# Two-layer transformer on one core: half of the second sequence's rows turned by VectorE and moved by DMA, and the last weights loaded later from another queue

## The chip, the core and the metric

The kernel runs on one core of a Trainium2 chip. The metric is the time of one execution on the device in microseconds (us); lower is better. The engines of the core run side by side and meet through semaphores: TensorE (PE in the profile; PEld is its load of stationary operands), VectorE (DVE), ScalarE (ACT), GpSimd (POOL) and SyncE (SP). SP and POOL each have a queue from which they issue DMA transfers in order; an instruction that waits holds up everything behind it on its own engine.

## What is computed

The input x is 2 sequences of 512 rows by 512 columns, in float32. Two layers follow, each an attention and a feed-forward, each with a residual and a layer norm behind it:

```
x = layernorm(x + L0_attn(x))     # linear attention, 8 key heads
x = layernorm(x + L0_ffn(x))      # ternary weights, 512 -> 1376 -> 512, int8 rounding
x = layernorm(x + L1_attn(x))     # this section is touched
x = layernorm(x + L1_ffn(x))      # down(silu(x gate) * (x up)), 512 -> 1376 -> 512

def L1_attn(x):                   # one head of width 128
    q, k, v = split(x @ Wqkv + bqkv)            # Wqkv is 512 x 384
    p = softmax(q @ k.T / sqrt(128))            # 512 x 512 for each sequence
    return (p @ v) @ Wo + bo
```

## The kernel before, in words

Every sequence is four tiles of 128 rows, `xs[b][t]` (b = 0, 1; t = 0 to 3), with the 512 columns along the free dimension. A product contracts over the partitions, so before every projection the rows have to be turned: x^T is held as four blocks k of 128 columns by 512 rows. The kernel turns rows in two ways.

- **On TensorE**: a 128x128 transpose against the identity, four to a PSUM bank, and then a copy of the bank to SBUF by ScalarE or VectorE (`transposed`, L128 to L130; L981 and L983).
- **In squares**: VectorE's transpose instruction turns each 32x32 square of a tile in place (`squares`), and `move_squares` (L305 to L322) then carries the squares to their places: for 16 pairs of 32-partition groups, 8 DMAs from SP (L316), 4 from POOL (L316), and the 4 on the diagonal, which stay in their partitions, as copies on VectorE (L320).

The stage of this study is where the second layer's attention begins, with the end of the first feed-forward ahead of it:

1. The first feed-forward's down products (L848) are finished row tile by row tile: ScalarE scales and truncates (L865, L170, L171), VectorE adds the residual (L881, L885) and takes the statistics (L138, L140), POOL makes the reciprocal root (`rstd`, L146 and L147), and VectorE applies the norm (L152, `normed`). Sequence 1's tiles come last, tile 3 at the very end.
2. Second attention, sequence 0: tiles 0 and 1 were turned in squares (L963 and L316), tiles 2 and 3 on TensorE (L981). `pqk` (L1148) makes q and k in two halves of 256 rows; `pv` (L1166) makes v, and VectorE adds its bias (L1172); `psc` (L1099) makes four tiles of scores; VectorE takes the maxima (L1105, L1106), ScalarE the exponentials `prob` (L1121), and VectorE turns those in squares (L1180), which are then moved (`pt_p`, L316).
3. Second attention, sequence 1: all four tiles are turned on TensorE (`pt_a`, L128, 16 transposes of 128x128) and copied by ScalarE and VectorE (L130); `pqk` runs over 512 rows at a time; then v, the scores and the exponentials.
4. `pot` (L1213, values times probabilities of sequence 0), `pt_p` (L128, the turning of sequence 1's probabilities on TensorE), `po` (L1230, the output projection of sequence 0), and so on into the last feed-forward (L1383, L1338).

The output projection bias `bo` is added to the rows ahead of the attention's result: for sequence 0 by POOL (L1181), for sequence 1 by accumulating DMAs from POOL's queue (L1196), which wait until `pt_p` has landed (L1194).

The last feed-forward's weights are `gu` (gate and up, chunks 0 to 10, 512 KB each, the last 384 KB) and `wd` (down, 11 chunks of 256 KB, the last 192 KB). All are loaded from SP's queue: `gu` 6 to 10 first, then, behind the moves of sequence 0's squares (`moves_a`), `wd` 0 to 10 (L256) and `gu` 0 to 5 (L245). The feed-forward uses them in the order 6, 7, 8, 9, 10, 0, 1, ... 5: ScalarE and VectorE split each chunk in parts (L1026, L1036, L1037) ahead of its products.

What sets the order: on ScalarE, VectorE, TensorE and SP a scheduler orders instructions by the program and by the ties written into it (`tc.issue_after(a)` holds the instructions under it behind `a`); POOL keeps the program's order. PSUM has eight banks, taken in turn (`psum(name)`, `bufs=8`): the ninth tile waits until the first has been read. The pool `xtp` has two slots of 128 x 2048 float32, tag `xt`, which sequence 1's turned rows, the turned probabilities (`xt_p1`) and the squares of the last feed-forward's rows (`squares_r1`) take in turn.

```
for half in range(2 - b):                 # L1140: q and k
    for j in range(2):
        for k in range(NK):
            if b: p, rows = pqk[j], xt[:, k, :]                       # 512 rows
            else: p = pqk[j].rearrange(...)[:, half]; rows = xt_a10[half][:, :, k, :]
            nc.tensor.matmul(p, wqkv[:, k, ts(j, D)], rows, ...)      # L1148
```

Of the kernel before, what the change touches and what calls it, by code (L numbers as in the profile page):

```python
# [10 lines left out]
F32 = mybir.dt.float32  # L11
# [8 lines left out]
P = 128  # L20
B, S, HID = 2, 512, 512
NT = S // P
# [17 lines left out]
def kernel(  # L40
# [195 lines left out]
    def branch(flag):  # L236
        return nc.values_load(flag[0:1, 0:1], engines=[PE], min_val=0, max_val=1)

    def up_weights(gu_in, name, chunks=range(len(CHUNKS))):
        gus = []  # L240
        for c in chunks:
            i, n = CHUNKS[c]
            gu = wffn.tile([P, 2, NK, n], F32, tag=f"gu{c}", name=f"gu{name}_{c}")
            at = 2 * HID * i
            nc.sync.dma_start(  # L245
                gu.rearrange("p a k i -> p (a k i)"),
                gu_in[at : at + 2 * HID * n].rearrange("(p f) -> p f", p=P),
            )
            gus.append(gu)
        return gus  # L250

    def down_weights(wd_in, name):
        wds = []
        for c, (i, n) in enumerate(CHUNKS):
            wd = wdp.tile([P, HID], F32, tag=f"wd{c}", name=f"wd{name}_{c}")
            nc.sync.dma_start(wd[:n], wd_in[i : i + n, :])  # L256
            if n < P:
                nc.gpsimd.memset(wd[n:], 0.0)
            wds.append(wd)
        return wds  # L260
# [497 lines left out]
    moved = move_squares(squares, xt1)  # L758
    wdp = ctx.enter_context(tc.tile_pool(name="wdp", bufs=1))
    with tc.issue_after(moved.ins):  # L760
        wds = down_weights(wd0_in, "0")
    with tc.tile_pool(name="f0", bufs=2) as f0:
        factors = {}

# [105 lines left out]
        def added(i, behind=(), late=(), first=()):  # L870
            b, t = order[i]
            with ExitStack() as tied:
                for step in behind:
                    tied.enter_context(tc.issue_after(step.ins))
                ta, tb = truncated_parts(f0, ys[i], P, f"d{i}")

            x = xs[b][t]
            with ExitStack() as tied:
                for step in first:
                    tied.enter_context(tc.issue_after(step.ins))  # L880
                nc.vector.scalar_tensor_tensor(x, tb, 128.0, x, ALU.min, ALU.subtract)  # L881
            with ExitStack() as tied:
                for step in late:
                    tied.enter_context(tc.issue_after(step.ins))
                taken[i] = nc.vector.scalar_tensor_tensor(x, x, -1.0, ta, ALU.mult, ALU.add)  # L885
            stats[i] = layernorm_stats(x, f"f0_{i}")
# [16 lines left out]
        def normed(i, behind=None):  # L903

            b, t = order[i]
            n = min(i + 1, len(order) - 1)
            if behind is None:
                behind = taken[n if t == NT - 1 else f"f0_{n}"]

            with tc.issue_after(behind.ins):  # L910
                norms.append(layernorm_apply(xs[b][t], xs[b][t], stats[i]))
            return norms[-1]
# [65 lines left out]
        for t in range(TURNED, NT):  # L978
            pt = psum(f"pt_a10_{t}")
            for k in range(NK):  # L980
                nc.tensor.transpose(pt[:, ts(k, P)], xs[0][t][:, ts(k, P)], ident)  # L981
            copies.append(
                nc.scalar.copy(xt_a10[1][:, t - TURNED], pt.rearrange("p (k i) -> p k i", k=NK))  # L983
            )
        added(i - 2)
        normed(i - 3)
        added(i - 1, behind=copies[-2:])
        normed(i - 2)
        for i in range(len(order), len(order) + 2):
            f0_down(i)  # L990

    def joined_weights(gu_in, c):

# [12 lines left out]
        nc.sync.dma_start(half.rearrange("p (k i) -> p k i", k=NK), up[:, :, : P // 2])  # L1006
        return full, half

    gus = up_weights(gu1_in, "1", range(6, len(CHUNKS) - 1))
    gus.append(joined_weights(gu1_in, len(CHUNKS) - 1))  # L1010
    with tc.issue_after(moves_a.ins):
        wds = down_weights(wd1_in, "1")
    gus = up_weights(gu1_in, "1", range(6)) + gus

# [73 lines left out]

    probs = []

    def scores(b):

        qt, kt, _ = qkv[b]
        got = []
        for t in range(NT):
            p = psum(f"psc_{b}_{t}")
            nc.tensor.matmul(p, qt[:, ts(t, P)], kt, start=True, stop=True)  # L1099
            got.append((p, small.tile([P, 1], F32, tag="mx", name=f"mx_{b}_{t}", bufs=8)))  # L1100

        def maxima(tiles):
            for t in tiles:
                p, mx = got[t]
                nc.vector.reduce_max(mx, p, AX.X)  # L1105
                done = nc.vector.tensor_scalar_mul(mx, mx, -scale)  # L1106
            return done

        return got, maxima
# [18 lines left out]
    qkv = []  # L1128
    for b in range(B):
        if b:  # L1130
            xt = transposed(xs[b], f"a1{b}")
            with tc.issue_after(copies[-2].ins), tc.issue_after(copies[-1].ins):
                split_up(0, room0)
                split_up(1, room1[:6])
        qk = []
        qk2 = query_tile(f"qk_{b}")
        if b == 0:
            v2 = query_tile("v")
        pqk = [psum(f"pqk_{b}_{j}") for j in range(2)]
        for half in range(2 - b):  # L1140
            for j in range(2):
                for k in range(NK):
                    if b:
                        p, rows = pqk[j], xt[:, k, :]
                    else:
                        p = pqk[j].rearrange("p (h t i) -> p h t i", h=2, i=P)[:, half]
                        rows = xt_a10[half][:, :, k, :]
                    nc.tensor.matmul(  # L1148
                        p, wqkv[:, k, ts(j, D)], rows,
                        start=(k == 0), stop=(k == NK - 1),  # L1150
                    )
        for j, p in enumerate(pqk):
            s = qk2[:, j, :]
            moved = nc.scalar.activation(s, p, AF.Identity, bias=bqk[:, j : j + 1])
            qk.append(s)
        if b:
            pt0 = fp.tile([P, NT, NK, P], F32, tag="it10", name="pt_p0", bufs=1)
            move_squares(squares, pt0)
            pt0 = pt0.rearrange("p t k i -> p k t i")
        else:  # L1160
            table(AF.Exp, moved)
        v = v2[:, b, :].rearrange("p (t d) -> p t d", t=NT)
        for t in range(NT):
            p = psum(f"pv_{b}_{t}")
            for k in range(NK):
                nc.tensor.matmul(  # L1166
                    p[:, :D],
                    xt[:, k, ts(t, P)] if b else xt_a10[t // 2][:, t % 2, k, :],
                    wqkv[:, k, ts(2, D)],
                    start=(k == 0), stop=(k == NK - 1),  # L1170
                )
            nc.vector.tensor_add(v[:, t, :], bv, p[:, :D])  # L1172
        qkv.append((qk[0], qk[1], v))
        if b == 0:
            got, maxima = scores(0)
            maxima(range(NT))
            exponentials(0, got)
            squares = fp.tile([P, NT, HID], F32, tag="it00", name="squares_p0", bufs=1)
            for t in range(NT):
                nc.vector.transpose(squares[:, t, :], probs[0][0][t])  # L1180
                nc.gpsimd.tensor_add(xs[0][t], xs[0][t], bo)  # L1181
# [364 lines left out]
    for i, (b, j) in enumerate(steps):  # L1546
        held.append(up1(b, j, held))
        finished = held[0][0]
        if i == AHEAD:
            with tc.issue_after(in_turn.last.ins), tc.issue_after(uppers.ins):  # L1550
                moved = finish_up()
        elif i > 1:
            while len(held) > 1:
                moved = finish_up()
        if i == 1:
            in_turn(lambda: split_up(AHEAD - 1, take(6)))
        elif i == 2:
            rooms[1] = rows_room(1, "r1")
            x3[1] = row_blocks(rooms[1])
            for k in range(NK):  # L1560
                with tc.issue_after(in_turn.last.ins):
                    uppers, in_turn.last = rows_from_squares(k)
        elif i == AHEAD:
            for h, m, d in x3[1]:
                in_turn(lambda: crossed(d, h, m))
        with tc.issue_after(moved.ins):
            if ahead <= last and finished == 1:
                split_up(
                    ahead, room0 if ahead == AHEAD else take(6 if turn[ahead] < last else 4)
                )  # L1570
                ahead += 1
            for _ in range(2):
                if len(down_parts) <= last and len(free) >= (15 if ahead <= AHEAD + 3 else 9 if ahead <= last else 3):
                    split_down()
        if (b, j) == (1, last - 1):
            quarters = [split_tile(0, 0)]
# [69 lines left out]
```

## Time and profile before

| | us |
|---|---|
| median of 4 runs | 454.68 |
| lowest and highest of them | 454.58, 455.06 |
| the profiled execution | 454.54 |
| its span, first to last instruction | 452.8 |
| TensorE busy in it | 445.8 (98%) |
| VectorE, ScalarE, POOL busy | 318.0 (70%), 259.5 (57%), 118.1 (26%) |
| TensorE's share of the chain that ended last | 97% |

Times in the profile are counted from the start of the span. A line of the timeline gives the start, the length, the engine, the line of code, the operation and what it writes and reads, the count where several are merged, and in square brackets the idle time before it and what ended that. Float32 products appear as two TensorE instructions each, so a product of 128x512 counts twice ("x8" for four of them). The ends of TensorE's instructions are modelled, so one starts before the one ahead of it has drained; the chain of work gives net times.

### The profile page before, as it was taken

How to read it: one execution, taken by the hardware profiler on the slowest of the kernel's cores; microseconds unless marked ns; L12 is line 12 of the kernel's file. 1: busy time of each engine (PE TensorE's matmuls, PEld its weight loads, DVE VectorE, ACT ScalarE, POOL GpSimd, SP SyncE). 2: the span in 40 equal slices, each digit the busy share in tenths (PEclk: the TensorE clock that was granted, in tenths of full speed). 3: DMA queues.
4: the chain of work that ended last, by engine and by line, in shares of the span. 5: the costliest groups of instructions: out<-in, count | busy, mean ns of one | idle time of the engine just before them, and what ended most of it. 6: DMA issues, size and time to landing. Idle time of an engine off the chain costs nothing.

```text
span 452.8 us, 5850 instructions
## 1 busy us (share of the span) xinstructions
PE 445.8 (98%) x1913; PEld 337.1 (74%) x1913; DVE 318.0 (70%) x634; ACT 259.5 (57%) x493; POOL 118.1 (26%) x164
## 2 busy tenths in 40 slices
PE   8999999999999999999999999999999999999995
PEld 8887753444587888888885578888888888888884
DVE  3976757877886898859898889545535447777524
ACT  5788995567467975567755645454645456442311
POOL 0400206565640059203384137000000000012111
PEclk9999999999999999999999999999999999999999
DMA  8999980020038001132693503200000000000101
GB/s 305 396 265 314 190 306 7 0 46 4 1 58 262 5 2 48 48 94 46 185 371 73 90 1 51 43 0 1 0 1 0 0 3 0 0 25 23 48 25 68
DMA packets 35604, 38.57 MB, mean 85 GB/s; under 512 B 23024, under 2 KB 23920, under 8 KB 35568
## 3 DMA queue, kind: packets, MB, share of 16 engines
q1 hardware_dynamic: 32912, 31.31, 21.2%
q0 software_dynamic: 2368, 6.42, 7.7%
q8 instruction: 22, 0.36, 0.3%
q10 hardware_dynamic: 288, 0.36, 0.2%
q14 instruction: 14, 0.11, 0.1%
HBM read 32.45 MB, written 2.10 MB: 76 GB/s over the span
## 4 chain that ended last, share of the span: by engine, by line
PE 97%; issue 1%; DVE 0%; ACT 0%; POOL 0%; POOLq 0%
PE pu L1338 24%; PE po L593 12%; PE pd L1338 12%; PE pq L538 9%; PE pg_f L789 9%; PE pu_f L789 9%; PE pd_f L848 4%; PE pqk L1148 3%; PE pu L1383 2%; PE pv L1166 2%; PE pot L1213 2%; PE po L1230 2%; PE psc L1099 2%; PE pmw L579 2%; PE pq L509 1%
## 5 line engine op out<-in xcount | busy, mean ns | idle before, releaser
L593 PE MATMUL po<-mw,q 128*128 128x512 f32 x128 | 56.9, 598 | 0.0
L1338 PE MATMUL pu<-r,ugu 128*128 128x512 f32 x200 | 48.6, 389 | 0.0
L146 POOL TENSOR_TENSOR rstd_f<-mv_f,ln_eps 128x1 f32<-128x1 f32 x15 | 6.0, 397 | 161.8 <-DVE mv_f L1506 128.8
L364 ACT ACTIVATE pu<-pu 128x512 f32<-128x512 f32 x42 | 24.2, 580 | 41.4 <-PE pu L1338 37.6
L593 PEld LDWEIGHTS po<-mw,q 128*128 128x128 f32 x128 | 22.8, 189 | 32.5 <-issue 15.9
L1338 PEld LDWEIGHTS pu<-r,ugu 128*128 128x128 f32 x200 | 37.5, 188 | 7.8
L615 DVE SCALAR_TENSOR_TENSOR x<-po,den,x 128x511 f32<-128x511 f32 x40 | 29.8, 746 | 1.9
L170 ACT ACTIVATE ta_f<-y_f,below_half 128x512 int8<-128x512 f32 (+1 forms) x22 | 15.9, 722 | 24.6 <-DVE y_f L158 21.8
L610 POOL TENSOR_TENSOR y<-y,y 128x511 f32<-128x511 f32 x16 | 21.3, 1332 | 24.6 <-ACT y L606 23.9
L1338 PE MATMUL pu<-r,it_early 128*128 128x512 f32 x104 | 24.9, 389 | 0.0
L1397 DVE TENSOR_TENSOR it_f<-ev,pu 128x512 f32<-128x512 f32 x20 | 13.7, 684 | 15.7 <-PE pu L1338 15.4
L1226 ACT ACTIVATE x<-x,off_f,rstd_f 128x512 f32<-128x512 f32 x7 | 5.7, 816 | 31.6 <-POOL off_f L1225 31.6
L815 DVE SCALAR_TENSOR_TENSOR it_f<-tb_f,ta_f 128x512 fp32r<-128x512 int16 (+1 forms) x22 | 15.6, 707 | 11.1 <-ACT tb_f L171 11.1
L1338 PEld LDWEIGHTS pu<-r,it_early 128*128 128x128 f32 x104 | 19.5, 188 | 4.1
L1338 PE MATMUL pd<-ugu,r 128*128 128x512 f32 (+1 forms) x79 | 22.5, 362 | 0.0
L789 PE MATMUL pg_f<-x,tu 128*128 128x512 f32 x88 | 22.1, 393 | 0.0
L789 PE MATMUL pu_f<-x,tu 128*128 128x512 f32 x88 | 21.7, 389 | 0.0
L376 POOL TENSOR_SCALAR td<-wd,inv_down 128x512 fp32r<-128x512 f32 x11 | 20.4, 1872 | 3.2 <-DVE inv_down L206 3.2
L848 PE MATMUL pd_f<-td,it_f 128*128 128x512 f32 x88 | 20.3, 389 | 0.0
L597 ACT ACTIVATE den<-po,den_eps 128x1 f32<-128x1 f32 x64 | 14.1, 272 | 10.6 <-PE po L593 10.5
L789 PEld LDWEIGHTS pg_f<-x,tu 128*128 128x128 f32 x88 | 16.4, 188 | 4.0 <-DVE x L615 0.4
L789 PEld LDWEIGHTS pu_f<-x,tu 128*128 128x128 f32 x88 | 16.5, 188 | 3.5
(396 smaller groups left out, 1118.5 us busy)
## 6 DMA issues: line engine op xcount, KB each, us to landing
gu<-in_gu SPq DMA_DIRECT2D x20, 512.0 KB, 6.7
wd<-in_wd SPq DMA_DIRECT2D x20, 256.0 KB, 5.4
wo<-in_wo SPq DMA_DIRECT2D x8, 512.0 KB, 8.6
wo<-in_wo POOLq DMA_DIRECT2D x8, 512.0 KB, 9.4
wq<-in_wq SPq DMA_DIRECT2D x8, 256.0 KB, 4.5
x<-in_x SPq DMA_DIRECT2D x7, 256.0 KB, 4.4
out<-x SPq DMA_DIRECT2D x7, 256.0 KB, 2.0
x<-in_bo POOLq DMA_DIRECT2D x4, 256.0 KB, 6.1
```

What stands on the lines that cost most here:

```text
L170: nc.scalar.activation(a[:n], y, AF.Relu, bias=below_half[:n])
L364: return nc.scalar.activation(p, p, AF.Copy, scale=BIG + 1.0)
L376: eng.tensor_scalar(out, w, factor, None, ALU.mult)
L538: done = nc.tensor.matmul(p, w, x, start=(start and i == 0), stop=(i == len(todo) - 1), skip_group_check=not start,)
L593: nc.tensor.matmul(po, qs[b][h0 + j][:, ts(t, P)], mw[:, h0 + j, :], start=True, stop=True,)
L597: nc.scalar.activation(den[:, j : j + 1], po[:, LAST:], AF.Identity, bias=den_eps)
L610: nc.gpsimd.tensor_add(ys[0][:, :LAST], ys[0][:, :LAST], y[:, :LAST])
L615: steps.append(nc.vector.scalar_tensor_tensor(x[:, :LAST], four[j][:, :LAST], d, x[:, :LAST], ALU.mult, ALU.add))
L789: nc.tensor.matmul(pp[a], t[:, a, i % NK, :], x2[b][i], start=(i == 0), stop=(i == 2 * NK - 1),)
L815: nc.vector.scalar_tensor_tensor(it[:n], tb[:n], 128.0, ta[:n], ALU.min, ALU.subtract)
L848: nc.tensor.matmul(pd, inter[b][c][:, ts(t, P)], td[c].bitcast(F32R), start=(c == 0), stop=(c == last),)
L1338: done = nc.tensor.matmul(p, w, x, start=(start and i == 0), stop=(i == n - 1), skip_group_check=not start,)
```

## The change

It does two things.

First, sequence 1's tiles 0 and 1 are turned in squares by VectorE inside the end of the first feed-forward, each behind the norm of its tile, and `move_squares` carries them to `xt_a11` (8 DMAs from SP, 4 from POOL, 4 copies on VectorE). Tiles 2 and 3 are still turned on TensorE, 8 transposes instead of 16, but earlier: between the first and the second score tile of sequence 0 (`turn_others`), with both copies on ScalarE. The q and k products of sequence 1 then run in two halves of 256 rows, tiles 2 and 3 first.

Second, of the last feed-forward's weights only `gu` 0 and 1 stay on SP behind the moves (now the moves of sequence 1's squares); `gu` 2 to 5 and all of `wd` are issued from POOL's queue, inside the last feed-forward, behind a small POOL copy `landed_r1` that waits for the last block of sequence 1's turned rows.

```diff
@@ end of the first feed-forward
+        squares_a = xtp.tile([P, NT, HID], F32, tag="xt", name="squares_a11")
+        xt_a11 = xtp.tile([P, NT, NK, P], F32, tag="xt", name="xt_a11")
         added(i - 2)
-        normed(i - 3)
+        last_norm = normed(i - 3)
+        with tc.issue_after(last_norm.ins):
+            done = nc.vector.transpose(squares_a[:, 0, :], xs[1][0])
         added(i - 1, behind=copies[-2:])
-        normed(i - 2)
+        with tc.issue_after(done.ins):
+            last_norm = normed(i - 2)
+        with tc.issue_after(last_norm.ins):
+            nc.vector.transpose(squares_a[:, 1, :], xs[1][1])
         for i in range(len(order), len(order) + 2):
             f0_down(i)
+        moves_a = move_squares(squares_a[:, :TURNED], xt_a11[:, :TURNED])
@@ the last feed-forward's weights
-    gus = up_weights(gu1_in, "1", range(6, len(CHUNKS) - 1))
+    gus = [None] * 6 + up_weights(gu1_in, "1", range(6, len(CHUNKS) - 1))
     gus.append(joined_weights(gu1_in, len(CHUNKS) - 1))
     with tc.issue_after(moves_a.ins):
-        wds = down_weights(wd1_in, "1")
-    gus = up_weights(gu1_in, "1", range(6)) + gus
+        gus[:2] = up_weights(gu1_in, "1", range(2))
@@ second attention
+    def turn_others(t):
+        if t != 1:
+            return
+        for t in range(TURNED, NT):
+            pt = psum(f"pt_a11_{t}")
+            for k in range(NK):
+                nc.tensor.transpose(pt[:, ts(k, P)], xs[1][t][:, ts(k, P)], ident)
+            copies.append(nc.scalar.copy(xt_a11[:, t], pt.rearrange("p (k i) -> p k i", k=NK)))
...
         if b:
-            xt = transposed(xs[b], f"a1{b}")
...
-        for half in range(2 - b):
+        xt = [xt_a11[:, :TURNED], xt_a11[:, TURNED:]] if b else xt_a10
+        for half in (1, 0) if b else (0, 1):
...
-            got, maxima = scores(0)
+            got, maxima = scores(0, turn_others)
@@ last feed-forward, behind the split of sequence 1's rows
+            landed = small.tile([P, 1], F32, tag="off", name="landed_r1")
+            nc.gpsimd.tensor_copy(landed[:SQ], x3[1][NK - 1][0][:SQ, S - 1 :].bitcast(F32))
+            gus[2:6] = up_weights(gu1_in, "1", range(2, 6), nc.gpsimd)
+            wds = down_weights(wd1_in, "1", nc.gpsimd)
```

The order of the changed kernel's instructions, which the scheduler fixes when the kernel is built, is this. VectorE: the transpose of tile 0 stands right behind the residual of tile 2 (L885), the transpose of tile 1 right behind that of tile 3, and one of the four diagonal copies ahead of tile 3's last statistics, three behind its norm, all ahead of the v additions of sequence 0. ScalarE: the two new copies stand ahead of the first exponential; three of the splits of the first weights stand between the first and the second exponential, where they stood behind the fourth. POOL: the four moves stand behind the last reciprocal root and ahead of the `bo` additions. TensorE: as told above, with no other move. From the output projection on, all engines but POOL and SP have the order that they had.

More of the change, by code (lines that the diff above doesn't have):

```diff
@@ L237, in branch, with up_weights @@
         return nc.values_load(flag[0:1, 0:1], engines=[PE], min_val=0, max_val=1)
-    def up_weights(gu_in, name, chunks=range(len(CHUNKS))):
+    def up_weights(gu_in, name, chunks, eng=nc.sync):
         gus = []
@@ L244, in up_weights @@
             at = 2 * HID * i
-            nc.sync.dma_start(
+            eng.dma_start(
                 gu.rearrange("p a k i -> p (a k i)"),
@@ L250, in up_weights, with down_weights @@
         return gus
-    def down_weights(wd_in, name):
+    def down_weights(wd_in, name, eng):
         wds = []
@@ L255, in down_weights @@
             wd = wdp.tile([P, HID], F32, tag=f"wd{c}", name=f"wd{name}_{c}")
-            nc.sync.dma_start(wd[:n], wd_in[i : i + n, :])
+            eng.dma_start(wd[:n], wd_in[i : i + n, :])
             if n < P:
@@ L760 @@
     with tc.issue_after(moved.ins):
-        wds = down_weights(wd0_in, "0")
+        wds = down_weights(wd0_in, "0", nc.sync)
     with tc.tile_pool(name="f0", bufs=2) as f0:
@@ L1091, with scores @@
     probs = []
-    def scores(b):
+    def turn_others(t):
[6 more added lines that the diff above has]
+            copies.append(nc.scalar.copy(xt_a11[:, t], pt.rearrange("p (k i) -> p k i", k=NK)))
+    def scores(b, between=lambda t: None):
         qt, kt, _ = qkv[b]
@@ L1097, in scores @@
         for t in range(NT):
+            between(t)
             p = psum(f"psc_{b}_{t}")
@@ L1139 @@
         pqk = [psum(f"pqk_{b}_{j}") for j in range(2)]
-        for half in range(2 - b):
+        xt = [xt_a11[:, :TURNED], xt_a11[:, TURNED:]] if b else xt_a10
+        for half in (1, 0) if b else (0, 1):
             for j in range(2):
                 for k in range(NK):
[L1143 to L1147, printed above, removed]
+                    p = pqk[j].rearrange("p (h t i) -> p h t i", h=2, i=P)[:, half]
+                    rows = xt[half][:, :, k, :]
                     nc.tensor.matmul(
@@ L1167 @@
                     p[:, :D],
-                    xt[:, k, ts(t, P)] if b else xt_a10[t // 2][:, t % 2, k, :],
+                    xt[t // TURNED][:, t % TURNED, k, :],
                     wqkv[:, k, ts(2, D)],
```

## The prediction

> **What bounds the kernel.** I read the page's busy shares first (TensorE 98%), then TensorE's waits over the whole span:
>
> ```profile
> engine line waited for: us in total, times, longest us
> PE rise L113 <- DVE below_half L108: 1.1, 1, 1.1
> PE pq L509 <- ACT xt_raw L484: 0.2, 1, 0.2
> ```
>
> TensorE waits 1.3 us in all, at the very start. From then until 441.9 us it never stops, so the time falls only by TensorE work that is taken away, and rises by any wait that is put in. Next, the chain of work from 215 to 275 us, which gives net times:
>
> ```profile
> 221.13 0.87 PE pt_a L981 x8
> 222.01 6.91 PE pqk L1148 x32
> 228.92 3.57 PE pv L1166 x32
> 232.49 3.44 PE psc L1099 x8
> 235.92 1.75 PE pt_a L128 x16
> 237.67 7.03 PE pqk L1148 x16
> 244.70 3.57 PE pv L1166 x32
> 248.27 3.44 PE psc L1099 x8
> 251.71 3.43 PE pot L1213 x8
> 255.14 1.75 PE pt_p L128 x16
> 256.88 3.44 PE po L1230 x8
> ```
>
> The lines at 235.92 and 237.67, sequence 1's transposes and its q and k, are what the change touches; sequence 0 has the same work in the new form at 221.13 and 222.01.
>
> **What is taken away.** Sixteen transposes cost 1.75 us (235.92). Eight stay, and eight cost 0.87 us (221.13): **-0.88 us**. The q and k products over 512 rows took 7.03 us, in halves of 256 rows they took 6.91 us for sequence 0: **-0.12 us**. Together -1.00 us, and nothing else is removed from TensorE, so this is the most that the change can bring. All the rest is whether TensorE comes to wait. I walk the changed order through the old durations; times without a row are estimates made in this way.
>
> **VectorE up to the last norm.** These rows of VectorE's timeline end the first feed-forward:
>
> ```profile
> 230.36 0.18 DVE L140 BATCH_NORM_AGGREGATE mv_f<-st_f 128x2 f32<-128x6 f32 x1
> 230.46 0.52 DVE L152 TENSOR_SCALAR x<-x,mv_f,rstd_f 128x512 f32<-128x512 f32 x1
> 231.69 0.83 DVE L152 TENSOR_SCALAR x<-x,mv_f,rstd_f 128x512 f32<-128x512 f32 x1 [0.71 <-POOL rstd_f L147]
> 232.44 0.86 DVE L1172 TENSOR_TENSOR v<-bv,pv 128x128 f32<-128x128 f32 x4
> ```
>
> From 223.3 us to the 0.71 us wait shown here VectorE has no gap. The change puts in two transposes (0.62 us apart where others follow) and one diagonal copy (1.17 us for four at 213.01, so 0.29): 1.53 us. The last norm, which waits for POOL's root of the last statistics, starts at 231.69 + 1.53 = 233.2 and takes 0.52 to 0.83 (the longer beside a POOL fill): tile 3 is ready at 233.7 to 234.1. TensorE now asks for it after one score tile (0.86) and the transposes of tile 2 (0.44): 232.49 + 1.30 = 233.8. Wait: **0 to 0.3 us**. POOL's addition for the root took 0.19 to 1.60 us in this stage; the long one (226.45) would add 1.3 us. The same position in the order took 0.34, so I keep it, and keep 1.3 for the range.
>
> Three more copies (0.87) put the v additions at 232.44 + 1.53 + 0.87 = 234.8. The third score tile takes the PSUM bank of the first v product: it wants it at 235.1, and the addition is done at 235.1. **0 to 0.1 us**, and not on top of the wait before, which moves both.
>
> **The moves of the new squares.** They issue when the second transpose ends: 227.32 plus 0.62 + 0.61 + 0.60 + 0.09 + 0.43 + 0.60 + 0.70 (the instructions between, by their spacing) = 231.0. The rows for the same moves of sequence 0, and for the probabilities' squares:
>
> ```profile
> 212.81 6.11 SPq L316 DMA_DIRECT2D xt_a<-squares_a x8
> 239.54 5.34 SPq L316 DMA_DIRECT2D pt_p<-squares_p x8
> ```
>
> So SP issues until 237.1, and the last, issued at 236.5, lands 2.1 us later by the median of those moves (1.9 to 3.5): 238.6, at worst 240.0; the longest landing of any such move is 5.7 us, which would be 242.2. POOL's four (2.40 us, 2.5 to landing) start behind the last root, 233.2, and land by 238.1. TensorE needs them after the first half: 235.92 + 0.87 + 3.46 = 240.25. **Nothing, by 1.6 us**; at the worst landing +1.9 us. The cover is that half 1, from TensorE's own transposes, goes first.
>
> The weights matter here: SP issued `wd` and `gu` from 219.0 to 229.7, and the DMA engines were busy 0.95 of the stretch from 219 to 236 us. Without 15 of these 17 loads the moves find them free; hence I take the median landing.
>
> The Trainium skill speaks against such moves. In "VectorE: DVE Perf Modes", section "The three transpose paths", it warns that a transpose made by a plain strided DMA copy is many times slower than the hardware one, and its rules send a 128x128 transpose to TensorE. The trace agrees as to length (8 us from squares to landing against 0.87 us for the eight transposes); by the rule the sum would be no gain. But here it is TensorE's time that is short.
>
> **What comes later on VectorE.** The v additions are 2.4 us later than before, the two bank copies of sequence 1 (L130, 1.2 us by spacing) are gone, and three weight splits (0.53 us each) now stand between ScalarE's first and second exponential. Walking maxima (0.73 to 0.86 a tile), exponentials and transposes, the squares of the first probabilities are done at 242.5, where they were at 239.5. They were landed 6.9 us after that:
>
> ```profile
> 246.46 0.18 POOL L1194 COPY landed<-pt_p 32x1 f32<-32x1 f32 x1 [4.04 <-DMA pt_p<-squares_p]
> ```
>
> so 249.4 now; `pot` wants them at 251.71 - 1.00 = 250.7. **Nothing, by 1.3 us.**
>
> VectorE reaches the maxima of sequence 1 at about 249.2 (seven splits, the diagonal copies and v behind 242.5), as before (249.17); there TensorE set the time, now VectorE does. So ScalarE's rows behind them stay where they are while TensorE comes 1.00 us earlier:
>
> ```profile
> 253.45 1.28 ACT L1089 ACT_TABLE_LOAD   x1
> 255.38 0.56 ACT L1218 COPY ot<-pot 128x512 f32<-128x512 f32 x1
> ```
>
> `po` needs that copy: it ends at 255.94 and TensorE would ask at 256.88 - 1.00 = 255.88. **0 to 0.4 us**, since the walk is good to some 0.3 us; again not on top of the wait for tile 3, which delays both. I take 0.2 us for these three waits together.
>
> **The weights.** Fifteen issues leave SP (11 `wd` in 6.07 us, 4 of 6 `gu` in 2.9) and go to POOL at 0.66 to 0.91 us each (its rows for 4 moves and for 4 `bo` loads): 10 to 14 us from about 290.5, where POOL is busy 1.04 us between 291 and 320. Behind them stand a fill of `wd` and two of `it_f` (302.66 before), read only by the down products after 385. POOL's queue moved 6.42 MB in 7.7% of the span, 184 GB/s, so 4.9 MB need some 27 us, the first chunk 9.4 us (the 512 KB loads from POOL). First reads: `gu` 2 at 314.0, 3 at 324.7, `wd` at 345.9. **Nothing, by over 12 us.** POOL's `bo` additions (5.02 us) move to 235.6 and end at 240.7, read at 257.85; the accumulating `bo` loads land by 259.3, read after 263.6. Nothing.
>
> From `po` on each step is released by TensorE and moves with it. The sum: 454.54 (this execution; its span of 452.8 and 1.7 around it) - 1.00 + 0.20 = 453.7. The median of the runs is 0.14 higher than the profiled execution: **453.9 us**.
>
> **Rivals.** One measurement of this kernel tells about 0.2% from nothing, 0.91 us: faster means below 453.77, slower above 455.59.
>
> - *All waits are nil, or a little more is won* (the 512-row products or the transposes also cost hidden gaps): 453.5 to 453.77. For it: every margin above is positive or within 0.1 us. Against it: ScalarE's copy for `po`, which no longer has slack. 25%.
> - *Forecast*: one small wait of 0.1 to 0.5 us stays: 453.77 to 454.2. 40%.
> - *The gain is eaten*: POOL's root takes the long 1.60 us, or a move lands at 3.5 to 5.7 us: waits of 0.5 to 1.9 us, 454.2 to 455.6; for the root alone 454.68 - 1.00 + 1.3 = 455.0. For it: one root in five here was that slow. Against it: those stood beside the loads that now are gone. 20%.
> - *Slower*: the probabilities' squares. They are done 3 us later and TensorE wants them 1 us earlier, and `gu` 0 and 1 (1 MB) were issued just ahead of them on the same queue. It decides when they land later than 252.6, that is 10.1 us after the squares instead of 6.9. The row of the last feed-forward's squares (277.36 to at most 283.1 + 5.7 = 288.8) gives 11.4: 253.9, a wait of 3.2 us and 456.9. Against it: that one has twice POOL's moves, and 1 MB takes 3 us at the 328 GB/s of this stage. 15%.
>
> A wait above some 3.4 us would, by the skill's "TensorE: Matmul & The Clock Gate", section "The HAM clock gate", also halve TensorE's clock for a while; no case here reaches it, and the granted clock is 1.00 in every stretch from 219 to 320 us.
>
> Range: 453.5 to 455.2 holds the first two cases, most of the third: some 8 in 10. Faster 0.25, same 0.40 + 0.20 = 0.60, slower 0.15.
>
> **What would show it.** Right: in the chain, 8 transposes of about 0.87 us between two score tiles, q and k of sequence 1 near 6.9 us, `po` of sequence 0 starting 0.6 to 1.0 us earlier than 256.88; in TensorE's waits at most small rows at the transposes of tile 3 and at `po`. Wrong: a TensorE wait for DMA at the second half of q and k or at `pot`; the first weight splits from POOL's loads waiting for DMA after 313; `po` no earlier than before.

## The result, and the profile after

The changed kernel takes **455.57 us** (median of 35 runs, 454.73 to 456.23), the kernel before 454.69 us (55 runs, 454.11 to 456.22). The ratio is 1.0017, with a 95% interval of 1.0012 to 1.0022: 0.55 to 1.0 us slower, where 0.8 us faster was forecast. The profiled execution of after took 455.51 us, with a span of 453.7 us.

The stage that the change touches did what the prediction said. TensorE's waits over the whole span of after, in the columns that were explained for before:

```profile
engine line waited for: us in total, times, longest us
PE rise L113 <- DVE below_half L108: 1.1, 1, 1.1
```

No wait has been added. The chain of after in that stage (start, us, engine, what it writes, line, count):

```profile
221.50 0.87 PE pt_a L981 x8
...
232.85 0.86 PE psc L1117 x2
233.71 0.91 PE pt_a L1107 x8
234.62 2.58 PE psc L1117 x6
237.20 6.91 PE pqk L1163 x32
...
256.29 3.44 PE po L1245 x8
```

Eight transposes of 0.91 us stand between two score tiles, and q and k of sequence 1 take 6.91 us. From the transposes of sequence 0 to `po` it is 256.29 - 221.50 = 34.79 us, against 256.88 - 221.13 = 35.75 before: **0.96 us gained**. (Both start late or early by what happens in the first 220 us; so only differences within an execution are used below.) The gain is still there at the end of the chain. Its last lines, first of before, then of after:

```profile
448.35 0.89 POOLq L1642
449.24 0.02 issue
449.26 0.46 ACT x L1516
```

```profile
447.77 0.89 POOLq L1662
448.66 0.02 issue
448.69 0.46 ACT x L1531
```

ScalarE starts the last piece of the output 228.13 us behind the transposes of sequence 0 in before (449.26 - 221.13) and 227.19 us in after: 0.94 us less. But the chain of work stops there, and the span does not. From that start to the end of the span it is 452.760 - 449.264 = 3.50 us in before, and 453.722 - 448.688 = 5.03 us in after (the trace holds the times in ns; the page rounds the spans to 452.8 and 453.7). **The loss, 1.54 us, lies wholly behind the last computation.** What stands there is the closing of the program. The instructions of the last line of the code, one row each from before and from after (duration in ns, minimum/median/maximum, and when the first and the last start):

```profile
L1642 POOLq DRAIN  x3: 46/107/3592, 448.3 to 452.5; - x3
```

```profile
L1662 POOLq DRAIN  x3: 46/98/5143, 447.8 to 453.4; - x3
```

The first of POOL's three drains, with which the program waits until POOL is empty, starts beside POOL's last instruction (the root of the last tile's variance, 0.84 us) and takes 3.59 us in before, 5.14 us in after: 1.55 us more. In both the span ends 0.81 to 0.82 us behind the end of that drain (452.76 - 451.94, 453.72 - 452.91). POOL computes the same at the end. What it has more in its history is DMAs: by the profile's list of DMA issues 32 come from POOL's queue in before (8 of `wo`, 4 of `bo`, 20 moves of squares), and 51 in after (4 more moves, 15 weight loads).

So the account of the traces is -0.94 + 1.54 = +0.60 us, inside the measured +0.55 to +1.0 us, but 0.3 us below the difference of the medians; that is taken up at the end. The TensorE clock is not the cause: the granted clock is 1.00 in both from 0 to 220, 220 to 260 and 260 to 450 us.

### The profile page after: what moved, and what is told of

It is laid out like the page before. It is cut to its first block, busy times and chain, and to the rows that moved or that the text cites. A ratio compares the mean times of both kernels' runs of the same rounds, so it can differ in the third digit from the quotient of the medians.

```text
span 453.7 us, 5902 instructions
## 1 busy us (share of the span) xinstructions
PE 445.5 (98%) x1921; PEld 339.9 (75%) x1921; DVE 317.9 (70%) x638; ACT 259.4 (57%) x493; POOL 128.3 (28%) x184
## 4 chain that ended last, share of the span: by engine, by line
PE 97%; issue 1%; DVE 0%; POOL 0%; POOLq 0%; ACT 0%
PE pu L1353 24%; PE po L593 12%; PE pd L1353 12%; PE pq L538 9%; PE pg_f L789 9%; PE pu_f L789 9%; PE pd_f L848 4%; PE pqk L1163 3%; PE pu L1398 2%; PE pv L1181 2%; PE pot L1228 2%; PE psc L1117 2%; PE pmw L579 2%; PE po L1245 2%; PE pq L509 1%; PE rise L113 1%
## 5 line engine op out<-in xcount | busy, mean ns | idle before, releaser
L593 PE MATMUL po<-mw,q 128*128 128x512 f32 x128 | 56.9, 598 | 0.0
L593 PEld LDWEIGHTS po<-mw,q 128*128 128x128 f32 x128 | 22.8, 189 | 32.5 <-issue 15.9
```

Source lines behind the costliest of these rows:

```text
L593: nc.tensor.matmul(po, qs[b][h0 + j][:, ts(t, P)], mw[:, h0 + j, :], start=True, stop=True,)
```

## Theory and rivals

**Theory**: the closing drain of POOL grows with the DMAs that POOL has issued, whenever that was; 15 of the 19 new ones are the late weights. It is open at first whether number, packets or bytes count: 1.55 us for 19 DMAs, 1568 packets or 5.05 MB. **Rival 1**: the late loading itself costs, by a collision or a late read. **Rival 2**: after's later start of the stage (221.50 against 221.13) is systematic. **Rival 3**: the turning costs, by its moves or its order.

In the table, "stage" is the time from the transposes of sequence 0 to the last output's work on ScalarE, "tail" from there to the end of the span, both of the profiled execution; "POOL DMAs" are those issued from POOL's queue. Ratios are to the kernel before on the same chip, with the 95% interval.

| kernel | POOL DMAs | drain | stage | tail | ratio |
|---|---|---|---|---|---|
| before | 32 | 3.592 | 228.13 | 3.50 | |
| before, again | 32 | 3.590 | 228.13 | 3.49 | |
| after | 51 | 5.143 | 227.19 | 5.03 | 1.0017 (1.0012 to 1.0022) |
| after, again | 51 | 5.142 | 227.15 | 5.03 | 0.9997 (0.9985 to 1.0009) |
| turning alone | 36 | 3.918 | 227.53 | 3.81 | 1.0005 (0.9993 to 1.0017) |
| late weights alone | 47 | 4.815 | 228.64 | 4.71 | 1.0029 (1.0018 to 1.0039) |
| late weights on SP | 36 | 3.917 | 227.16 | 3.81 | 0.9982 (0.9969 to 0.9996) |
| after, last root left out | 51 | 4.580, early | 226.83 | 3.42 | 0.9959 (0.9944 to 0.9974) |
| after, a drain at 302 us | 51 | 0.957 | 227.18 | 3.41 | **0.9961 (0.9946 to 0.9976)** |
| before, 19 tiny DMAs more | 51 | 5.143 | 228.13 | 5.03 | 1.0038 (1.0024 to 1.0051) |

## Experiments: whose tail is it

**The turning alone.** All weights go back to SP, in the order of the kernel before.

```diff
     with tc.issue_after(moves_a.ins):
-        gus[:2] = up_weights(gu1_in, "1", range(2))
+        wds = down_weights(wd1_in, "1", nc.sync)
+    gus[:6] = up_weights(gu1_in, "1", range(6))
...
-            gus[2:6] = up_weights(gu1_in, "1", range(2, 6), nc.gpsimd)
-            wds = down_weights(wd1_in, "1", nc.gpsimd)
```

> The turning alone: the kernel after, with all weights loaded by SP at the place and in the order of the kernel before. 36 POOL DMAs. Theory: drain 3.7 to 3.9 us as with the weights late on SP; if the moves of the new squares, now beside the weight loads, still land before the second half of q and k, 454.2 to 454.4 us; if they land late, TensorE shows a wait for DMA at that half or at the products of the probabilities, of 0.5 to 3 us, and the time is higher by it. Rival 1 (late loading costs the time): 454.2 here, against 455.5 with the weights late on SP. Rival 3 (the four extra moves or the order around the third score tile cost the time): 455.4 to 455.6.

455.38 us, against 455.44 for the kernel before on that chip, where 0.3 to 0.5 us less was expected. The drain came as the theory said, but the stage gained only 0.60 us instead of 0.94. In the chain `pot` stands behind a late maximum of VectorE:

```profile
250.69 0.61 DVE mx L1124
251.30 3.66 PE pot L1229 x8
```

VectorE keeps pace with after up to a split of a weight chunk at 240.25 us, and comes out of it 0.67 us late. This is that row, and below it the same one of after:

```profile
240.25 1.71 DVE L1044 SCALAR_TENSOR_TENSOR it_early<-it_early,gu 128x512 fp32r<-128x512 f32 x1
```

```profile
240.20 1.09 DVE L1043 SCALAR_TENSOR_TENSOR it_early<-it_early,gu 128x512 fp32r<-128x512 f32 x1
```

A split of the same form took 0.68 us alone, in after at 245.41. Both long ones end 0.55 us after the last of POOL's additions of `bo`, which ran from 236.46 to 241.41 here and from 235.78 to 240.74 in after. They stand later here because POOL's fill of `wd` (0.52 us, at 235.85) is ahead of them again. SP was free of its weight loads at 242.05; it issued the moves of the first probabilities at 243.21 instead of 242.54 because VectorE had done the squares later.

By the traces the turning alone is worth -0.60 + 0.32 = -0.28 us, which the ratio (0.9993 to 1.0017) doesn't tell from nothing. By the traces too, the late loading does not cost in the stage, it is worth 0.34 us more there: it keeps that fill off the additions. So Rival 1 falls for the kernel after, and with it rival 3: the turning gains in the stage with the weights in either place.

**The late weights alone.** The kernel before, with `gu` 2 to 5 and `wd` issued late by POOL and the transposes of sequence 1 left on TensorE.

```diff
+            landed = small.tile([P, 1], F32, tag="off", name="landed_r1")
+            nc.gpsimd.tensor_copy(landed[:SQ], x3[1][NK - 1][0][:SQ, S - 1 :].bitcast(F32))
+            gus[2:6] = up_weights(gu1_in, "1", range(2, 6), nc.gpsimd)
+            wds = down_weights(wd1_in, "1", nc.gpsimd)
```

> The other half alone: the kernel before, with gu chunks 2 to 5 and all of wd loaded late by POOL as in the kernel after; the transposes of sequence 1 stay on TensorE. 47 POOL DMAs. Theory: compute ends as in the kernel before, drain 4.8 us (by number) to 5.0 us (by packets), time 1.2 to 1.4 us above the kernel before, 455.9 to 456.1. Rival 3 (it is the turning, not the weights, that costs): 454.6 to 454.8, same as before. Rival 1 (late loading) also gives a slower kernel, but with TensorE waits or a drain that is no longer than 3.6 us.

456.96 us, 1.5 above the kernel before. The drain of this kernel, 15 DMAs more than before:

```profile
L1646 POOLq DRAIN  x3: 46/98/4815, 449.5 to 454.8; - x3
```

The tail grew by 1.21 us, where the theory asks for 15 x 0.082 = 1.22. The stage grew by 0.51 us, which nobody had asked. VectorE's norm of sequence 1's last tile, which took 0.83 us in before, is this row here:

```profile
232.29 1.48 DVE L152 TENSOR_SCALAR x<-x,mv_f,rstd_f 128x512 f32<-128x512 f32 x1 [0.71 <-POOL rstd_f L147]
```

In before, POOL's fill of `wd` (0.52 us) stood ahead of its additions of `bo`; with the loads the fill went away too, the additions began 10.49 us into the stage instead of 11.18 (232.23 - 221.74 against 232.31 - 221.13), and the norm ran beside them. VectorE was that much later at the copy of the turned rows, for which TensorE waits 0.3 us at `pqk`. In the kernel after this doesn't happen, because the additions stand later, at 235.78.

**The late weights on SP.** The same place, the other queue. A first try tied the `gu` loads to VectorE's split of the rows instead of to a step on SP, and the `wd` loads to nothing. The scheduler put one `wd` ahead of the moves of sequence 0's squares, and four `gu` and five more `wd` ahead of the moves of the new squares.

> The kernel after, with the fifteen late weight loads issued by SP instead of POOL at the same point of the program (four late gu chunks and all of wd, behind the second split of sequence 1's rows). Theory (POOL's closing drain grows with the DMAs that POOL has issued; 5.14 us after 51 of them, 3.59 us after 32): 36 POOL DMAs are left, so the drain is 3.9 us by their number or 3.7 us by their packets, the compute ends as in the kernel after, and the time is 454.2 to 454.4 us, 0.3 to 0.5 below the kernel before. Rival 1 (it is the late loading itself, by what it collides with or reads late): still 455.4 to 455.6, with the drain anything. Rival 2 (the 0.37 us by which the profiled execution of after was late before any changed instruction is systematic): 455.3 to 455.6 with a short drain.

That kernel took 461.02 us, and TensorE's waits show why (after's one row had no such line):

```profile
PE pqk L1163 <- DMA xt_a<-squares_a: 4.1, 1, 4.1
```

These are not the new squares: `xt_a` names the turned rows of both sequences, and the wait stands ahead of the first q and k, those of sequence 0. SP's first `wd` load waited for the first feed-forward's down products, and the eight moves behind it were issued at 219.76 instead of 213.17 us:

```profile
SPq L256 <- PE pd_f L848: 11.2, 1, 11.2
```

```profile
219.31 0.34 SPq L256 DMA_DIRECT2D wd<-in_wd  x1
219.76 5.17 SPq L316 DMA_DIRECT2D xt_a<-squares_a  x8
```

```profile
226.56 8.83 PE L1163 MATMUL pqk<-xt_a,wqkv 128*128 128x256 f32 x32 [4.13 <-DMA xt_a<-squares_a]
```

Behind the wait these products took 8.83 us instead of 6.91, and the granted clock was 0.61 from 226 to 230 us, where it is 1.00 in before and after: the fall of the clock that the prediction named for long waits. The 4.1 and 1.9 us, less what the turning gains, are about the 5.6 us that this kernel lost. It says nothing about the late loading. Of the new squares it shows that with the nine loads just ahead of them their moves landed 2.5 to 6.6 us after their issue, the last at 240.2 us (after: 1.9 to 2.3 us, 237.8); TensorE, late itself, did not wait for them. Its drain was 3.918 us for 36 DMAs. Then with the loads behind SP's last move of sequence 1's rows:

```diff
-    move_squares(squares, xt_r1, queues=2)
+    moved_r1 = move_squares(squares, xt_r1, queues=2)
...
+            with tc.issue_after(moved_r1.ins):
+                gus[2:6] = up_weights(gu1_in, "1", range(2, 6))
+                wds = down_weights(wd1_in, "1", nc.sync)
```

> The kernel after, with the fifteen late loads on SP behind its last move of sequence 1's rows (about 289 us), so that they are neither on POOL nor ahead of the new squares' moves. 36 POOL DMAs. Theory: no TensorE wait, compute as in the kernel after, drain 3.918 us as in the two kernels that have 36 such DMAs, tail 1.2 us shorter: 1.2 us below the kernel after, 0.3 to 0.4 us below the kernel before. If the late loading itself costs: no faster than the kernel after. If the order on SP's queue was not the cause of the 4.1 us wait for the new squares: that wait again.

454.59 us, 0.8 below the kernel before (by the traces -0.97 in the stage and +0.32 in the tail, -0.65). The stage is that of after (227.16), the tail 1.22 us shorter. The loads are late here too (issued from 284.5 to 294.8 us, in after from 290.6 to 301.4), and what differs in the time is the tail: the queue is the price.

**After and before once more**, on the chip of that run.

> The kernel after once more, unchanged, on the chip of the next three. Theory: drain 5.14 us as before, the compute ends as much earlier as it did, some 0.8 us slower than the kernel before, 1.6 us slower than the same kernel with an early drain. The start of the second attention (eight transposes of sequence 0) came 0.37 us later than in the profiled execution of before; if that is one execution's chance, it falls anywhere in 221.1 to 222.5 here, beside the copy of the kernel before.

> The kernel before once more, unchanged, for a second profiled execution of it. By chance alone: the eight transposes of sequence 0 start anywhere within 221.1 to 222.5 us; if the changed kernel's late start there is systematic, at 221.0 to 221.3 and below that of the kernel after on this chip. Drain 3.59 us in either case.

Stage, drain and tail repeat to 0.04 us. The stage now starts at 220.76 us in after and at 221.75 in before, the other way round: rival 2 falls, the start goes either way. The time itself did not repeat: after came out at 455.44 against 455.37 us, where 0.8 us more was expected, and the interval (0.9985 to 1.0009) does not meet that of the first comparison (1.0012 to 1.0022). The start of the stage may be what moves such medians; that was not shown. From the two profiled executions of each the change is worth -0.96 to the stage and +1.54 to the tail.

## Experiments: what the drain counts, and how to be rid of it

**The last root left out**, so that POOL is done one tile earlier.

```diff
-            nc.gpsimd.tensor_tensor(rstd, mv[:, 1:2], minus_half, ALU.pow)
+            nc.vector.tensor_scalar(rstd, mv[:, 1:2], 0.0, 1.0, ALU.mult, ALU.add)
```

> The kernel after, with the root of the last tile's variance left out: VectorE writes ones in its place, so the last 128 rows of the output are not divided by their standard deviation. POOL's last instruction is then the root of the tile before, some 3.4 us earlier; the weights stay on POOL, 51 DMAs. Theory: the drain is as long as before (4.3 us behind the last instruction) but starts 3.4 us or more earlier, and is over at about 449; the end is set by the landing of the last output (issued some 0.5 us earlier, 448.6, landing 2 us later) and the closing barrier, 0.8 us: span 451.5 to 452, time 453.2 to 453.8. Of the gain some 0.5 us is the shorter tail of VectorE, over 1 us is the drain. Rival (the drain waits for something at the end of the program, and not only for POOL's own work): the drain's end moves by no more than 0.6 us, 454.9 to 455.1.

453.98 us, 1.5 below the kernel before. The drain is still long, but it starts 3.8 us earlier in the stage (445.0 - 222.46 against 447.8 - 221.50):

```profile
L1662 POOLq DRAIN  x3: 46/98/4580, 445.0 to 452.4; - x3
```

It ends at 449.6, before the last output is even issued (449.70), and the tail falls to 3.42 us. So the drain waits for POOL alone, and the floor below it is the landing of the output: 3.42 us, which before had almost reached with 3.50.

**Nineteen tiny DMAs.** The kernel before, with nineteen DMAs from POOL that move next to nothing. The first form wrote them into a new tile of 1216 bytes; beside it, one DMA with 1536 elements of 4 bytes went into a new tile of 96 bytes.

```diff
+                dump = small.tile([1, 19, 16], F32, tag="dump", name="dump", bufs=1)
+                for j in range(19):
+                    nc.gpsimd.dma_start(dump[:, j], bo_in[:, 16 * j : 16 * j + 16])
```

> The kernel before with nineteen DMAs of 64 bytes each from POOL's queue, behind the last split of sequence 1's rows (about 290 us), into a tile that nothing reads: as many as the change adds, with next to no bytes. If the closing drain grows with the number of DMAs (82 ns each): 3.59 + 19 x 0.0815 = 5.14 us, compute as in the kernel before, tail 1.4 to 1.5 us longer, 1.3 to 1.5 us above the kernel before. If with their packets or bytes: drain 3.6 us, time as the kernel before.

> The kernel before with one DMA from POOL's queue at the same place that takes 1536 separate elements of 4 bytes. If the closing drain grows with the number of DMAs: 3.59 + 0.08 = 3.67 us, time within 0.1 us of the kernel before. If with packets or descriptors (1 ns each by the difference of the two kernels): 5.1 us, 1.4 us above the kernel before.

460.60 and 461.15 us, 6.1 and 6.6 us above the kernel before, which neither reading had. The drains are clear all the same: 5.142 us for the nineteen, and for the one of 1536 elements

```profile
L1650 POOLq DRAIN  x3: 46/107/3675, 454.3 to 458.6; - x3
```

that is 3.592 + 0.083. **The drain counts DMAs**, not what they carry. Most of the loss was in TensorE's products, with no wait shown: the last output's work on ScalarE starts 4.5 and 6.0 us later than in before. So the nineteen were put into slots of a tile that the kernel has anyway, and a third kernel had the new tile of 96 bytes without any DMA.

```diff
+                    dump = small.tile([P, 1], F32, tag="off", name=f"dump_{j}")
+                    nc.gpsimd.dma_start(dump[:1], bo_in[:, j : j + 1])
```

> The nineteen small DMAs again (4 bytes each), but each into a slot of a tile that the kernel has anyway, so that no other tile's address moves. In the two kernels with a new tile the closing drain was as the number of DMAs says (5.14 us for 19 more, 3.67 us for one more), yet TensorE took some 5 to 6 us more in all, without any wait; the new tile of 1216 or 96 bytes had moved all tiles above it off the 128-byte steps on which they stand in the kernel before. If that was the cause: the last output's work starts 228.1 us behind the transposes of sequence 0, as in the kernel before, drain 5.14 us, 1.3 to 1.5 us above the kernel before. If the DMAs themselves slow TensorE: 5 to 6 us above it again.

```diff
+                dump = small.tile([P, 24], F32, tag="dump", name="dump", bufs=1)
+                nc.gpsimd.memset(dump[:1], 0.0)
```

> The kernel before with a new tile of 96 bytes that POOL fills once on one partition, and no DMA more: the tiles above it move by 96 bytes. If the addresses slow TensorE: 5 to 7 us above the kernel before, with a drain of 3.59 us and no TensorE wait. If it was the DMAs: within 0.3 us of the kernel before.

The first took 456.51 us, 1.7 above the kernel before, with before's stage to the hundredth (228.13) and this drain:

```profile
L1647 POOLq DRAIN  x3: 46/102/5143, 448.9 to 454.6; - x3
```

Nineteen DMAs of 4 bytes make exactly the drain that the change made with 4 moves and 4.9 MB of weights. The second took 461.49 us, with a drain of 3.592 us: the 6 us come from the addresses (below).

Over all kernels but the one without the last root and the one that follows, with a drain in the middle, the closing drain is 0.98 us + 0.0816 us for each POOL DMA: 3.59 for 32, 3.67 for 33, 3.92 for 36, 4.82 for 47, 5.14 for 51. In all of them the span ends 0.81 to 0.83 us behind it.

**A drain in the middle.** The kernel after, with one instruction more.

```diff
             wds = down_weights(wd1_in, "1", nc.gpsimd)
+            nc.gpsimd.drain()
```

> The kernel after with one instruction more: a drain of POOL behind the last weight load and its fill, at about 302 us, where POOL has little else to do until 385. If the closing drain settles, once, for each DMA issued since the last drain (82 ns each): the new drain takes about 4.3 us at 302, and the closing one is short (0.84 us for the root under way, then well under 1 us); the end is set by the output's landing as in the kernel whose last root was left out, 1.4 to 1.6 us below the kernel after, 0.5 to 0.8 us below the kernel before, 453.9 to 454.2 on a chip where that takes 454.7. If the closing drain goes over all DMAs of the program each time: closing drain 5.1 us, time as the kernel after. If it costs per program start of something else than DMAs, also as the kernel after.

**453.82 us, 0.9961 of the kernel before (0.9946 to 0.9976)**, the version that beats both. The new drain and the closing one:

```profile
L1583 POOLq DRAIN  x1: 7472/7472/7472, 302.6 to 302.6; - x1
```

```profile
L1663 POOLq DRAIN  x3: 34/98/957, 449.2 to 453.3; - x3
```

The closing drain is down to the root under way (0.84) and 0.1 us more, and the tail to 3.41: the backlog is settled once, and each drain starts the count anew. Against after on the same chip the time fell by 1.62 us (455.44 to 453.82), and the tail by 1.62. By the traces this kernel is 0.95 + 0.08 = 1.0 us below the kernel before, by the interval 1.1 to 2.5. The new drain holds POOL until 310.1, where only the two fills of `it_f` stand behind it (two together, at 310.11), read after 385. It took 7.47 us, not the 4.3 us that were expected: 51 x 0.0816 is 4.2, and 1.0 until the fill ahead of it ended at 303.65 makes 5.2. The last load, issued at 302.56, landed 5.3 us later, at 307.9, some 2 us ahead of the drain's end at 310.04; what the drain did from then on stays open.

## Why the prediction was wrong

Step by step:

- **Taken away, -1.00 us**: right. The transposes went from 1.75 to 0.91 us, q and k from 7.03 to 6.91: -0.96.
- **Waits, 0.2 us**: none came. After's stage starts 0.37 us later than before's, so its times are given here less 0.37. Tile 3's norm started at 232.93 (233.2 was walked) and took 0.55 us; v's additions at 234.43 (234.8); the moves of the first probabilities were issued from 242.17 (242.5); the maxima of sequence 1 stood at 248.78 (249.2); `ot` was done at 255.33 (255.94), and `po` started at 255.92. The walk was 0.3 to 0.6 us late at each step. All three waits that were weighed stayed at nothing, the case that was given 25%.
- **The moves hidden by 1.6 us**: right, and with more room. The last landed at 237.8, and TensorE came to them at 237.20 + 3.46 = 240.66, 2.9 us later. That the weights ahead of them matter is right too: with nine loads just ahead, in the first try on SP, the last landed at 240.2.
- **"The weights ... Nothing, by over 12 us"**: the failed step. As issues it was right: 4 `gu` and 11 `wd` occupied POOL from 290.58 to 301.4, and no product waited for them. But it priced a POOL DMA by its issue and its landing alone. Each has a third price, 0.082 us in POOL's closing drain: 15 x 0.082 = 1.22 us. The Trainium skill's "DMA: Bandwidth & Descriptors", section "Issuing engines are not separate DMA queues", says that starting DMAs from several engines at once saves only the sequencer's time to initiate them; the runs here show that the engine which issues has this other effect, and they decide.
- **The moves on POOL**: four more at 0.082 us, 0.33 us that the prediction did not have either.
- **"From `po` on each step is released by TensorE and moves with it"**: right up to the last output's issue, which came 0.94 us earlier in the stage, and wrong behind it. The sum took the last 3.5 us of the span, and the 1.7 us around it, as fixed. In before they nearly were: the drain ended 0.2 us behind the landing of the output (451.94, 451.76), with 0.08 us between 3.50 and the floor of 3.42 us. So almost all of the 1.55 us was to be paid, and moving TensorE earlier moved the drain with it but did not shorten it.

With these terms the sum would have been 454.54 - 0.96 + 1.54 = 455.12, and 455.3 on the median. The measured median is 455.57. A single execution differs by more than that in the start of the kernel: the stage began anywhere from 220.76 to 222.96 us in the ten profiled executions of the table's kernels. Whether the 0.3 us belong to the change stays open; the second comparison, 0.9997, points the other way.

The rivals of the prediction all asked what TensorE would come to wait for. None asked what stands behind the last computation.

## What to carry to other kernels

The chain of work can end before the span does: compare the two, and ask which row of the program's closing lasts longest before taking the rest as fixed. DMAs issued from POOL's queue have, beside issue and landing, a price at the end of the program (here 0.082 us each, whatever their size and however early); it is paid as soon as POOL's drain ends later than the output lands. A drain put in where POOL is idle, or SP's queue for what can wait, takes it away: here 0.4% and 0.2% below the kernel before by the medians, 1.0 and 0.65 us by the traces.

## What the runs showed of the hardware beside that

**Addresses.** A tile of 96 bytes that only POOL fills, once, made the kernel 6.7 us slower (1.0148, 1.0132 to 1.0163). With a tile of 1216 bytes it was 6.1 us, of which 1.5 are the nineteen DMAs' drain. What such a tile changes, besides the fill, is where the tiles above it lie: 96 bytes further, or 64 bytes beside a step of 128. No view shows the addresses, nor where the tiles stood before; that they are the cause is concluded, since the nineteen DMAs without a new tile lost nothing in the stage. Two windows of 40 us in the last feed-forward (TensorE busy and its instructions, weight loads, VectorE, ScalarE, POOL, clock, DMA), first of before, then with the 96 bytes:

```profile
300.00:340.00 40.00, 40.00 (x178) 33.11 (x177) 19.42 (x31) 20.07 (x36) 1.04 (x2) 1.00 0.00 1
```

```profile
300.00:340.00 40.00, 40.00 (x174) 32.34 (x173) 19.27 (x31) 20.68 (x37) 1.04 (x2) 1.00 0.00 0
```

TensorE is busy all the time at the same granted clock, without a wait, and gets 174 products done instead of 178. By the mean of a group, the products `pu` (L1338, from `ugu`) took 394 ns instead of 389, while those of the first attention's output (L593, 598 ns) and of q and k (L1148, 454 ns) were as before. Which operand's address does it, and whether 64 or 128 bytes are the step that counts, wasn't tried. The Trainium skill's "SBUF — State Buffer", section "Operand start alignment", gives a rule for which addresses are legal and says that it is not about speed; these runs point to a speed side.

**POOL beside VectorE.** The same norm of 128x512 on VectorE took 0.52 us alone, 0.83 us when it began beside a fill on POOL and 1.48 us beside POOL's additions. A small fill ahead of those additions had been keeping them off it. A weight split on VectorE took 0.68 us alone, and 1.09 and 1.71 us beside the same additions, where a later start of them made it longer.
